# Graph layer with linear attention and 16 experts: opening loads in order of need, the attention's division in halves, scale and bias folded into W1, output stores on SyncE, early weights between their rows

## The chip, the cores and the metric

The kernel runs on one core of a Trainium2 chip. The metric is the device time of one execution in microseconds (us), lower is better. Engines are named as the profile names them: PE (TensorE matmuls), PEld (its weight loads), DVE (VectorE), ACT (ScalarE), POOL (GpSimd) and SP (SyncE, which here only issues DMAs).

## The reference

`x` has 3125 nodes of 256 features; there are 53125 edges, sorted by target; there are 16 experts with 512 hidden features, and each node goes to two of them. Cut to what matters:

```python
xn = layernorm(x)
# 1. graph: every node sums its weighted neighbours
agg = segment_sum(edge_weight[:, None] * xn[src], dst)          # 3125 x 256
gnn = agg @ gnn_W.T + gnn_b
# 2. mixer: linear attention over all nodes, 8 heads of 32
Q, K, v = elu(xn @ Wq) + 1, elu(xn @ Wk) + 1, (xn @ Wv) / N
KV  = einsum('shd,shv->hdv', K, v)
Z   = 1 / (einsum('lhd,hd->lh', Q, K.sum(0)) + 1e-6)
msg = layernorm((einsum('lhd,hdv,lh->lhv', Q, KV, Z) * N) @ Wm) * g1 + b1
h   = relu(concat([xn, msg]) @ W1) @ W2
mix = layernorm(h) * g2 + b2
x = x + gnn + xn + mix
# 3. experts: top 2 of 16, renormalised
y = layernorm(x)
p = softmax(y @ gate_w + gate_b); weights of the two largest, divided by their sum
out = x + sum over the two experts of weight * ((silu(y @ w1[e]) * (y @ w2[e])) @ w3[e])
```

## The kernel before

The nodes are cut into 25 tiles of 125 nodes (128 rows with padding). All of x lies in SBUF as `x_all` from the opening to the end, and results are added into it. PE does almost all of the work, in this order of stages:

1. **Opening and row tiles** (0 to about 116 us). One loop over the 25 tiles. `normed(t + 1)` normalises the next tile on DVE (`xn`, L408), transposes it on PE (L417) and copies it to `xnT` on ACT (L418). `projected(t)` multiplies by `wcat` (gnn_W, Wk and Wv side by side; L426, L428), forms `k_sb` with two ACT operations and one of DVE (L434), and stores the projected neighbours' rows `y`. `summed(t - 1)` adds K times v into `pkv` (L450). The loads of x come in six batches (`LOADS`), the moments and reciprocal roots in four (`BATCHES`; `rsqrt` is 14 small DVE instructions in a chain).
2. In the same loop a generator `windows()` is advanced piece by piece: it finds, for each five target nodes, where their edges begin, gathers a window of 128 edges each (indirect DMAs issued by POOL), and turns them into `keys` and `wgts`, with DVE work on 125x640 elements per piece. `LISTS` says after the `xn` of which tile how many pieces are taken. The piece that needs the gathered windows begins with the cast to `src_f` (L282).
3. From tile `HOT` on, `adjacency()` builds dense pieces of the adjacency matrix from keys and weights: a compare (`one`, L331) and a product (`wone`, L336) on DVE, 12 matmuls on PE (L351), a copy on ACT (L354), a store to HBM (`adj_d`) from SP.
4. **End of the KV sum and the mixer groups** (about 116 to 580 us). The tiles are taken in seven groups of four or three. `asked()` is a generator for the queries of one group: two projections (L466) with exp and relu, then the sums for the division (`ksum`, L476), an ACT copy (L478), the reciprocal (L479) and the product (L480) on DVE. `mixer()` then multiplies by `kvw` (L616), normalises on DVE (`mw`, L624), transposes (L628), applies the scale g1 and the bias b1 on ACT while copying to `mT` (L630), multiplies by `w1` (L639) and `w2` (L650). `queries[g + 1]` is advanced inside group g, and between the steps of a group the loop at the end adds `adjacencies` and `messages` (the products of the stored adjacency with y, L600), as many as `groups` says: (tiles, adjacencies, messages).
5. **Last messages and routing** (about 580 to 720 us). `last_messages(t)` adds the last part of the neighbours (L715, L717) and stores the rows of x to `out` (L719, issued by ACT). Gates and routing of batches of tiles run between them (`gate`: the transposed copy xT on ACT, L773, and the logits, L776, L777). `early_blocks()` gives the first six blocks of experts' work their lists, asks for the first weights (`wt`) and gathers their rows (`xb`) from POOL.
6. **Experts** (about 720 to 1047 us). Blocks of up to 256 lanes: rows gathered, transposed (L964) and copied (`xTb`, L967), multiplied (L978), silu and product (L985), L1004, and added to `out` by indirect DMAs of POOL (L1008).

Each engine executes its instructions in order. The order is chosen when the kernel is built, by a scheduler that follows the dependencies and the `issue_after` marks in the code; one instruction that waits holds back everything behind it on its engine. DMAs issued by one engine's queue start in the order of issue. The pool `a_ps` has PSUM tiles under the names "big" (two buffers) and "tok" (three).

Of the kernel before, what the change touches and what calls it, by code (L numbers as in the profile page):

```python
# [55 lines left out]
LISTS = {1: 1, 6: 1, 7: 2, 8: 2, 13: 1, 14: 1, 15: 1}  # L56
AHEAD = {1: (2, 5), 2: (5, 9), 3: (9, 12), 4: (12, 15), 6: (15, 17), 9: (17, 21), 10: (21, 25)}
HOT = 17
# [4 lines left out]
def tile_gps_layer(ctx: ExitStack, tc: tile.TileContext, a: dict, out: bass.AP):  # L63
# [12 lines left out]

    def row_bcast(src, n, name, pool=const):
        t = pool.tile([P, n], F32, name=name)
        nc.gpsimd.dma_start(t, bass.AP(tensor=src.tensor, offset=src.offset, ap=[[0, P], [1, n]]))
        return t  # L80
# [18 lines left out]
    def stats(mv, src):  # L99
        st = small.tile([P, 6], F32, name="bn_st")  # L100
        nc.vector.bn_stats(st, src)
        nc.vector.bn_aggr(mv, st)
# [18 lines left out]


# [6 lines left out]
    nc.gpsimd.memset(ones, 1.0)  # L129
    before = const.tile([V, V], F32, name="before")  # L130
# [31 lines left out]
    for batch in LOADS[1:3]:  # L162
        load_x(nc.sync, *batch)
    load_x(nc.scalar, *LOADS[3])
# [19 lines left out]
    nc.gpsimd.dma_start(g1, a["g1"])  # L184
    b1 = const.tile([128, 2], F32, name="b1")
    nc.gpsimd.dma_start(b1, a["b1"])
# [3 lines left out]
    nc.gpsimd.dma_start(gate_w, a["gate_w"].rearrange("(k p) e -> p k e", p=128))  # L190
    cb = w_mix.tile([P, C], F32, name="cb")
    nc.gpsimd.tensor_tensor(cb, b2, gnn_b, op=ALU.add)
# [33 lines left out]
    def windows():  # L226

        thr = prep.tile([V, GC], F32, name="thr")
        nc.gpsimd.iota(thr, pattern=[[GN * V, GC]], base=0, channel_multiplier=GN,
                       allow_small_or_imprecise_dtypes=True)  # L230
# [33 lines left out]
        for i in range(GC):  # L264
# [8 lines left out]
            nc.gpsimd.indirect_dma_start(out=win[:, i, :, :].rearrange("p e w -> p (e w)"), out_offset=None,  # L273
                                         in_=a["edges"][:, :],
                                         in_offset=bass.IndirectOffsetOnAxis(ap=start_i[:, at], axis=0))
            if i < GC - 1:
                yield
        nc.sync.dma_start(first_d.rearrange("(i r) o -> r (i o)", r=V), start_i)
# [106 lines left out]
    def deviations(t0, t1):  # L385
        ready[t0] = rsqrt(mv[:, t0:t1, 1], t1 - t0)
        nc.vector.tensor_scalar(by[:, t0:t1], ready[t0], 1.0, None, op0=ALU.add)
        nc.vector.scalar_tensor_tensor(less[:, t0:t1], mv[:, t0:t1, 0], -1.0, ready[t0], op0=ALU.mult, op1=ALU.mult)

    def moments(t0, t1):  # L390

        for i in range(t0, t1):
            stats(mv[:, i, :], x_all[:, i, :])
        for batch in BATCHES:
            if batch[1] == t1:
                deviations(*batch)

    pieces = windows()
    with tc.issue_after(next(pieces).ins):
        moments(*BATCHES[0])  # L400
    def normed(t):
# [8 lines left out]
        with tc.issue_after(ins.ins):  # L410
            for _ in range(LISTS.get(t, 0)):
                next(pieces, None)
            if t in AHEAD:
                moments(*AHEAD[t])
# [38 lines left out]
    groups = ((4, 4, 0), (4, 23, 5), (4, 23, 7), (4, 23, 7), (3, 23, 7), (3, 23, 7), (3, 23, 2))  # L453
# [3 lines left out]
    def asked(t0, nt):  # L457
# [5 lines left out]
        for c in range(2):  # L463
# [9 lines left out]
            yield  # L473
        for c in range(2):
            pz = a_ps.tile([128, 512], F32, name="big")
            nc.tensor.matmul(pz[:, :w], lhsT=ksum[:, c, :], rhs=qT[:, c, :w], start=True, stop=True)  # L476
            z = mix.tile([128, GROUP * P], F32, name="eq")
            nc.scalar.activation(z[:, :w], pz[:, :w], AF.Copy, bias=ATT_EPS / N, scale=1.0 / N)  # L478
            nc.vector.reciprocal(z[:, :w], z[:, :w])  # L479
            nc.vector.tensor_tensor(qT[:, c, :w], qT[:, c, :w], z[:, :w], op=ALU.mult)  # L480
            yield
# [5 lines left out]
    for t in range(NT):  # L487
# [10 lines left out]
        if t >= HOT:  # L498
            adjacencies(1 if t == HOT else 2)
# [21 lines left out]
    for c in range(2):  # L521
        pw = a_ps.tile([P, C], F32, name="tok", bufs=3)
        nc.tensor.matmul(pw, lhsT=kvT[:, c, :], rhs=wm[:, c, :], start=True, stop=True)
        nc.scalar.copy(kvw[:, c, :], pw)
    for _ in range(2):
        next(queries[1])
# [79 lines left out]
    def mixer(t0, nt, qT, following):  # L606
# [16 lines left out]
        for i in range(nt):  # L623
# [5 lines left out]
            for k in range(2):  # L629
                nc.scalar.activation(mT[:, k, i * P : (i + 1) * P], ptr[:, k, :], AF.Identity,  # L630
                                     bias=b1[:, k : k + 1], scale=g1[:, k : k + 1])
# [3 lines left out]
        for j in range(4):  # L635
# [5 lines left out]
            nc.scalar.activation(hT[:, j, :w], ph[:, :w], AF.Relu)  # L641
# [66 lines left out]
    def last_messages(t):  # L708
# [10 lines left out]
        nc.scalar.dma_start(out[t * V : (t + 1) * V, :], x_all[:V, t, :])  # L719
# [211 lines left out]
    SYNC = mybir.DependencyInfo(mybir.DependencyClass.Sync, mybir.DependencyReason.DATA)  # L931

    class Block:
# [8 lines left out]
        def rows(self):  # L942
            self.xb = ex.tile([LANES, 2, XW], F32, name="xb", bufs=4)
            for r in range(self.n):
                at = self.of[0][:, self.u + r : self.u + r + 1]

                tc.keep_in_program_order(nc.gpsimd.indirect_dma_start(
                    out=self.xb[:, r, :], out_offset=None, in_=self.given,
                    in_offset=bass.IndirectOffsetOnAxis(ap=at, axis=0)))

# [105 lines left out]
    def early_blocks():  # L1056
# [21 lines left out]
        behind = blocks[1].weights(nc.gpsimd, behind)  # L1078
# [10 lines left out]
        blocks[2].weights(nc.gpsimd, behind)  # L1089
        for block in blocks:  # L1090
            block.of = of
        for block in blocks[:4]:
            block.rows()
# [173 lines left out]
```

## Time and profile before

| | us |
|---|---|
| three runs | 1047.76, 1048.47, 1049.95 |
| median of the runs | 1048.47 |
| the profiled execution | 1049.14 |
| its span, first to last instruction | 1047.47 |
| PE busy | 1009.6 (96%) |
| DVE busy | 654.2 (62%) |
| ACT busy | 271.2 (26%) |
| POOL busy | 214.4 (20%) |
| mean granted clock of PE | 0.990 |

All durations and start times in the text come from the one profiled execution. "Granted clock" is the share of full speed that PE was given; "idle before <-releaser" names what ended an engine's idle time. Lines such as L434 are lines of the kernel before.

### The profile page before, as it was taken

What the parts mean: (1) busy time and instruction counts of PE and PEld (TensorE: products, weight loads), DVE (VectorE), ACT (ScalarE), POOL (GpSimd) and SP (SyncE); (2) the same over time, 40 slices, a digit from 0 to 9 for tenths busy, and PEclk for the clock granted to TensorE, in tenths of its full rate; (3) what the DMA queues carried; (4) which work ended last, traced back from release to release, by engine and by line L of the source; (5) the groups of instructions that cost most, each with busy time, mean ns of one, the idle gap of its engine ahead of it and who ended that gap; (6) DMA issues with size and microseconds to landing.
All of it is one profiled execution on the core that took longest, in us unless ns stands there. A gap on an engine that the chain in (4) does not pass through costs nothing.

```text
span 1047.5 us, 16216 instructions
## 1 busy us (share of the span) xinstructions
PE 1009.6 (96%) x5990; PEld 810.3 (77%) x5990; DVE 654.2 (62%) x1721; ACT 271.2 (26%) x588; POOL 214.4 (20%) x198
## 2 busy tenths in 40 slices
PE   7899999999999999999999999998999999999995
PEld 5567656686687787887877888887888888888884
DVE  8868589799698887965698248686942222222221
ACT  3466534223324232222142000103111111111110
POOL 5220000104110000000000001012545444445542
PEclk9899999999999999999999999999999999999998
DMA  8324103444343344443444555573756767677662
GB/s 227 74 96 172 61 31 120 143 140 148 116 140 142 121 161 151 167 176 140 143 181 142 175 165 159 166 263 118 201 161 182 246 203 222 183 219 220 196 203 27
DMA packets 70373, 165.08 MB, mean 158 GB/s; under 512 B 11091, under 2 KB 29934, under 8 KB 66314
## 3 DMA queue, kind: packets, MB, share of 16 engines
q1 hardware_dynamic: 50422, 134.24, 37.5%
q0 software_dynamic: 15520, 25.04, 10.6%
q10 hardware_dynamic: 4340, 4.64, 1.4%
q8 instruction: 50, 0.82, 0.3%
q14 instruction: 41, 0.34, 0.1%
HBM read 105.85 MB, written 58.00 MB: 156 GB/s over the span
## 4 chain that ended last, share of the span: by engine, by line
PE 72%; DVE 12%; issue 2%; ACT 1%; another core or an unknown queue 1%; DMA 0%; POOL 0%; ACTq 0%; POOLq 0%; DVEq 0%
PE ph L978 18%; PE pb L600 13%; PE po L1004 10%; PE big L639 7%; PE po L715 7%; PE pa L351 6%; PE tok L650 4%; DVE wone L336 2%; DVE one L331 1%; PE pa L600 1%; PE ptr L964 1%; PE big L466 1%; PE tok L616 1%; DVE wone L346 1%; PE big L476 1%
## 5 line engine op out<-in xcount | busy, mean ns | idle before, releaser
L978 PE MATMUL ph<-xTb,wt 128*128 128x256 f32 (+2 forms) x992 | 204.5, 355 | 3.4 <-ACT xTb L967 3.4
L978 PEld LDWEIGHTS ph<-xTb,wt 128*128 128x128 f32 x992 | 171.5, 190 | 27.4 <-ACT xTb L967 8.3
L600 PE MATMUL pb<-y_early,nbr 128*128 128x256 f32 x736 | 170.7, 382 | 0.4 <-DVE x_all L602 0.4
L336 DVE TENSOR_TENSOR wone<-one,wgts 128x1536 bf16<-128x1536 bf16 x150 | 141.7, 954 | 34.7 <-PE pa L351 34.5
L351 PEld LDWEIGHTS <-one 128*128 128x128 bf16 x1875 | 117.5, 97 | 40.9 <-issue 19.7
L600 PEld LDWEIGHTS pb<-y_early,nbr 128*128 128x128 f32 x736 | 135.4, 190 | 17.2 <-DVE x_all L602 1.0
L354 ACT COPY adj<-pa 128x512 f32<-128x512 f32 (+1 forms) x157 | 91.8, 586 | 185.7 <-PE pa L351 166.5
L351 PE MATMUL pa<-wone,one 128*128 128x128 bf16 x1875 | 130.6, 218 | 2.4 <-ACT adj L354 1.1
L985 DVE TENSOR_TENSOR hid<-hid,ph 128x512 f32<-128x512 f32 (+2 forms) x62 | 38.3, 618 | 144.8 <-PE ph L978 138.6
L1004 PE MATMUL po<-wt,hid 128*128 128x256 f32 (+1 forms) x456 | 115.2, 385 | 0.8 <-DVE yb L1007 0.8
L715 PE MATMUL po<-y_late,nbr 128*128 128x256 f32 x450 | 103.9, 385 | 0.5 <-DVE x_all L602 0.5
L331 DVE TENSOR_TENSOR one<-iota,keys 128x1024 bf16<-128x1024 bf16 x150 | 101.4, 696 | 0.6 <-POOL wgts L313 0.6
L1008 POOL DMA_INDIRECT out<-yb,to_l x45 | 70.9, 1575 | 114.6 <-DMA out<-yb,to_l 52.2
L715 PEld LDWEIGHTS po<-y_late,nbr 128*128 128x128 f32 x450 | 84.2, 192 | 11.4 <-DVE x_all L602 0.9
L1004 PEld LDWEIGHTS po<-wt,hid 128*128 128x128 f32 (+1 forms) x456 | 79.1, 184 | 17.6 <-DVE yb L1007 5.5
L984 ACT ACTIVATE hid<-ph 128x512 f32<-128x512 f32 (+2 forms) x62 | 33.6, 542 | 208.0 <-PE ph L978 206.1
L677 POOL TENSOR_TENSOR x_all<-x_all,cb 128x256 f32<-128x256 f32 x25 | 27.0, 1100 | 200.5 <-DVE x_all L602 145.5
L1007 DVE TENSOR_SCALAR yb<-po,sh 128x256 f32<-128x256 f32 (+1 forms) x57 | 27.5, 482 | 57.3 <-PE po L1004 55.3
L728 POOL IOTA rev<- 125x16 f32 x1 | 0.1, 149 | 296.6 <-DMA nbr<-adj_d 296.6
L426 PE MATMUL big<-wcat,xnT 128*128 128x512 f32 x100 | 49.4, 616 | 1.9 <-DMA wcat<-in_Wk 1.9
L639 PE MATMUL big<-xnT,w 128*128 128x512 f32 (+1 forms) x112 | 50.0, 559 | 0.7 <-ACT eq L478 0.7
L639 PE MATMUL big<-mT,w 128*128 128x512 f32 (+1 forms) x112 | 47.8, 549 | 1.8 <-ACT mT L630 1.8
(283 smaller groups left out, 1185.8 us busy)
## 6 DMA issues: line engine op xcount, KB each, us to landing
wt<-in_w SPq DMA_DIRECT2D x28, 1536.0 KB, 6.9
adj_d<-adj SPq DMA_DIRECT2D x156, 256.0 KB, 2.1
nbr<-adj_d SPq DMA_DIRECT2D x25, 576.0 KB, 4.3
nbr<-adj_d SPq DMA_DIRECT2D x50, 256.0 KB, 2.6
nbr<-adj_d SPq DMA_DIRECT2D x25, 512.0 KB, 3.4
wt<-in_w POOLq DMA_DIRECT2D x3, 1536.0 KB
out<-x_all ACTq DMA_DIRECT2D x25, 125.0 KB
xn_d<-rows POOLq DMA_DIRECT2D x4, 629.9 KB
```

Source lines behind the costliest of these rows:

```text
L331: nc.vector.tensor_tensor(one.rearrange("p b h e j -> p (b h) e j"), iota_2[:, None, :, :].to_broadcast(shape), ql.rearrange("p b h j -> p ...
L336: nc.vector.tensor_tensor(wone, one[:, :, 1:2, :, :].to_broadcast(shape), w[:, :, :, None, :].to_broadcast(shape), op=ALU.mult)
L351: nc.tensor.matmul(pa[:, j, :], lhsT=one[:, j // 2, 0, :, j % 2], rhs=wone[:, j // 2, i, :, j % 2], start=(i == 0), stop=(i == 2))
L354: copied = nc.scalar.copy(rows[:, :n, :], pa[:, :n, :])
L426: nc.tensor.matmul(pyk, lhsT=xnT[:, k, cols], rhs=wcat[:, k, : 2 * C], start=(k == 0), stop=(k == 1))
L600: nc.tensor.matmul(pb[:, i, :], lhsT=rows[:, k - t0, :], rhs=y_of(k), start=(k == t0 and i == 0), stop=(k == t1 - 1), skip_group_check=True)
L639: nc.tensor.matmul(ph[:, :w], lhsT=w1[:, k, j * 128 : (j + 1) * 128], rhs=rhs, start=(k == 0), stop=(k == 3))
L650: nc.tensor.matmul(po, lhsT=hT[:, j, i * P : (i + 1) * P], rhs=w2[:, j, :], start=(j == 0), stop=(j == 3))
L715: last = nc.tensor.matmul(pg, lhsT=rows[:, k - t0, :], rhs=y_of(k), start=(k == t0), stop=(k == t1 - 1))
L978: last = nc.tensor.matmul(p[:, m, :w], lhsT=self.wt[:, i, k * F + at : k * F + at + 128], rhs=self.xT[:, k, :w], start=(k == 0), stop=(k = ...
L1004: last = nc.tensor.matmul(po[:n_r, r, :], lhsT=self.hid[:, k, r * LANES : r * LANES + n_r], rhs=self.wt[:, 2, k * C : (k + 1) * C], start= ...
L1008: made.append(nc.gpsimd.indirect_dma_start(out=out[:, :], out_offset=bass.IndirectOffsetOnAxis(ap=at, axis=0), in_=yb[:n_r, r, :], in_offs ...
```

## The change

It has these parts:

- **Opening.** The seven loads of small constants and the sum `cb` on POOL are put in a list, and issued after the last window gather. `thr` is made early. The third and fourth batches of x are both issued by SP, and wait until the moments of the first two tiles are done (the fourth was on ACT's queue). `by` and `less`, two small factors, are computed after the first `xn` of a batch and not before it.
- **Lists.** The last three pieces of `windows()` come after tiles 14, 15 and 16 instead of 13, 14 and 15; `HOT` is 18 instead of 17, and every tile from there on has two adjacencies (tile 17 had one). The first mixer group has five adjacencies instead of four.
- **Division in halves.** `asked()` issues both sums first, and then works on the first two tiles (256 columns) of both halves of the features, then on the rest: ACT copy, reciprocal and product for each.
- **Scale and bias in W1.** After the KV sum, eight matmuls of one column compute `h_bias` (the lower half of W1 times b1), and POOL multiplies the lower half of `w1` by g1. `mT` is then one plain copy for each tile, and the relu takes `h_bias` as its bias.
- **Stores.** The 25 stores of the rows of x to `out` are issued by SP.
- **Early weights.** POOL issues the weights of block 1 after the rows of blocks 0 and 1, and those of block 2 after the rows of block 2.

```diff
 
-LISTS = {1: 1, 6: 1, 7: 2, 8: 2, 13: 1, 14: 1, 15: 1}
+LISTS = {1: 1, 6: 1, 7: 2, 8: 2, 14: 1, 15: 1, 16: 1}
 AHEAD = {1: (2, 5), 2: (5, 9), 3: (9, 12), 4: (12, 15), 6: (15, 17), 9: (17, 21), 10: (21, 25)}
-HOT = 17
+HOT = 18
 GROUP = 4
...
 
+    later = []
+
     def row_bcast(src, n, name, pool=const):
         t = pool.tile([P, n], F32, name=name)
-        nc.gpsimd.dma_start(t, bass.AP(tensor=src.tensor, offset=src.offset, ap=[[0, P], [1, n]]))
+        later.append((t, bass.AP(tensor=src.tensor, offset=src.offset, ap=[[0, P], [1, n]])))
         return t
...
     nc.gpsimd.memset(ones, 1.0)
+    thr = const.tile([V, GC], F32, name="thr")
+    nc.gpsimd.iota(thr, pattern=[[GN * V, GC]], base=0, channel_multiplier=GN, allow_small_or_imprecise_dtypes=True)
     before = const.tile([V, V], F32, name="before")
...
         nc.scalar.dma_start(wcat[:, :, i * C : (i + 1) * C], a[name].rearrange("(k p) o -> p k o", p=128))
-    for batch in LOADS[1:3]:
-        load_x(nc.sync, *batch)
-    load_x(nc.scalar, *LOADS[3])
+    load_x(nc.sync, *LOADS[1])
     wq = w_mix.tile([128, 2, C], F32, name="wq")
...
     g1 = const.tile([128, 2], F32, name="g1")
-    nc.gpsimd.dma_start(g1, a["g1"])
+    later.append((g1, a["g1"]))
     b1 = const.tile([128, 2], F32, name="b1")
-    nc.gpsimd.dma_start(b1, a["b1"])
+    later.append((b1, a["b1"]))
     g2 = row_bcast(a["g2"], C, "g2", w_mix)
...
     gate_w = const.tile([128, 2, NE], F32, name="gate_w")
-    nc.gpsimd.dma_start(gate_w, a["gate_w"].rearrange("(k p) e -> p k e", p=128))
+    later.append((gate_w, a["gate_w"].rearrange("(k p) e -> p k e", p=128)))
     cb = w_mix.tile([P, C], F32, name="cb")
-    nc.gpsimd.tensor_tensor(cb, b2, gnn_b, op=ALU.add)
 
...
 
-        thr = prep.tile([V, GC], F32, name="thr")
-        nc.gpsimd.iota(thr, pattern=[[GN * V, GC]], base=0, channel_multiplier=GN,
-                       allow_small_or_imprecise_dtypes=True)
         heads = prep.tile([V, V], F32, name="heads")
...
             nc.vector.tensor_copy(start_i[:, at], start_f[:, at])
-            nc.gpsimd.indirect_dma_start(out=win[:, i, :, :].rearrange("p e w -> p (e w)"), out_offset=None,
+            gathered = nc.gpsimd.indirect_dma_start(out=win[:, i, :, :].rearrange("p e w -> p (e w)"), out_offset=None,
                                          in_=a["edges"][:, :],
...
                 yield
+        with tc.issue_after(gathered.ins):
+            for place, what in later:
+                nc.gpsimd.dma_start(place, what)
+            nc.gpsimd.tensor_tensor(cb, b2, gnn_b, op=ALU.add)
         nc.sync.dma_start(first_d.rearrange("(i r) o -> r (i o)", r=V), start_i)
...
 
-    def deviations(t0, t1):
-        ready[t0] = rsqrt(mv[:, t0:t1, 1], t1 - t0)
-        nc.vector.tensor_scalar(by[:, t0:t1], ready[t0], 1.0, None, op0=ALU.add)
-        nc.vector.scalar_tensor_tensor(less[:, t0:t1], mv[:, t0:t1, 0], -1.0, ready[t0], op0=ALU.mult, op1=ALU.mult)
+    def factors(t0, t1, rstd):
+        nc.vector.tensor_scalar(by[:, t0:t1], rstd, 1.0, None, op0=ALU.add)
+        nc.vector.scalar_tensor_tensor(less[:, t0:t1], mv[:, t0:t1, 0], -1.0, rstd, op0=ALU.mult, op1=ALU.mult)
 
...
         for i in range(t0, t1):
-            stats(mv[:, i, :], x_all[:, i, :])
-        for batch in BATCHES:
-            if batch[1] == t1:
-                deviations(*batch)
+            found = stats(mv[:, i, :], x_all[:, i, :])
+        for t0, end in BATCHES:
+            if end == t1:
+                ready[t0] = rsqrt(mv[:, t0:t1, 1], t1 - t0)
+        return found
 
...
     with tc.issue_after(next(pieces).ins):
-        moments(*BATCHES[0])
+        found = moments(*BATCHES[0])
+
+    for batch in LOADS[2:4]:
+        tc.add_manual_dep(load_x(nc.sync, *batch).ins, found.ins.name, SYNC, reason="loads in the order of need")
+
     def normed(t):
...
         with tc.issue_after(ins.ins):
+            for batch in BATCHES:
+                if t == batch[0]:
+                    factors(*batch, rstd)
             for _ in range(LISTS.get(t, 0)):
...
 
-    groups = ((4, 4, 0), (4, 23, 5), (4, 23, 7), (4, 23, 7), (3, 23, 7), (3, 23, 7), (3, 23, 2))
+    groups = ((4, 5, 0), (4, 23, 5), (4, 23, 7), (4, 23, 7), (3, 23, 7), (3, 23, 7), (3, 23, 2))
     asked_for = []
...
             yield
+
+        pz = []
         for c in range(2):
-            pz = a_ps.tile([128, 512], F32, name="big")
-            nc.tensor.matmul(pz[:, :w], lhsT=ksum[:, c, :], rhs=qT[:, c, :w], start=True, stop=True)
-            z = mix.tile([128, GROUP * P], F32, name="eq")
-            nc.scalar.activation(z[:, :w], pz[:, :w], AF.Copy, bias=ATT_EPS / N, scale=1.0 / N)
-            nc.vector.reciprocal(z[:, :w], z[:, :w])
-            nc.vector.tensor_tensor(qT[:, c, :w], qT[:, c, :w], z[:, :w], op=ALU.mult)
+            p = a_ps.tile([128, 512], F32, name="big")
+            nc.tensor.matmul(p[:, :w], lhsT=ksum[:, c, :], rhs=qT[:, c, :w], start=True, stop=True)
+            pz.append((p, mix.tile([128, GROUP * P], F32, name="eq")))
+        for part in (slice(0, 2 * P), slice(2 * P, w)):
+            for c, (p, z) in enumerate(pz):
+                nc.scalar.activation(z[:, part], p[:, part], AF.Copy, bias=ATT_EPS / N, scale=1.0 / N)
+                nc.vector.reciprocal(z[:, part], z[:, part])
+                nc.vector.tensor_tensor(qT[:, c, part], qT[:, c, part], z[:, part], op=ALU.mult)
             yield
...
         if t >= HOT:
-            adjacencies(1 if t == HOT else 2)
+            adjacencies(2)
         last, *taken_on = projected(t)
...
         nc.scalar.copy(kvw[:, c, :], pw)
+
+    pb1 = a_ps.tile([P, C], F32, name="tok", bufs=3)[:, :4]
+    for j in range(4):
+        for k in range(2):
+            nc.tensor.matmul(pb1[:, j : j + 1], lhsT=w1[:, 2 + k, j * 128 : (j + 1) * 128], rhs=b1[:, k : k + 1],
+                             start=(k == 0), stop=(k == 1))
+    h_bias = w_mix.tile([128, 4], F32, name="h_bias")
+    nc.vector.tensor_copy(h_bias, pb1)
+    for k in range(2):
+        nc.gpsimd.tensor_scalar(w1[:, 2 + k, :], w1[:, 2 + k, :], g1[:, k : k + 1], None, op0=ALU.mult)
     for _ in range(2):
...
                 nc.tensor.transpose(ptr[:, k, :], mw[:, i, k * 128 : (k + 1) * 128], ident)
-            for k in range(2):
-                nc.scalar.activation(mT[:, k, i * P : (i + 1) * P], ptr[:, k, :], AF.Identity,
-                                     bias=b1[:, k : k + 1], scale=g1[:, k : k + 1])
+            nc.scalar.copy(mT[:, :, i * P : (i + 1) * P], ptr)
             yield
...
                                  start=(k == 0), stop=(k == 3))
-            nc.scalar.activation(hT[:, j, :w], ph[:, :w], AF.Relu)
+            nc.scalar.activation(hT[:, j, :w], ph[:, :w], AF.Relu, bias=h_bias[:, j : j + 1])
             yield
...
         stats(mv_g[:, t, :], x_all[:, t, :])
-        nc.scalar.dma_start(out[t * V : (t + 1) * V, :], x_all[:V, t, :])
+        nc.sync.dma_start(out[t * V : (t + 1) * V, :], x_all[:V, t, :])
         return last
...
         yield
-        behind = blocks[1].weights(nc.gpsimd, behind)
 
...
         of = yield from lists(col, EARLY_TILES, 2 * EARLY, "e")
-        blocks[2].weights(nc.gpsimd, behind)
         for block in blocks:
             block.of = of
-        for block in blocks[:4]:
-            block.rows()
+        for block in blocks[:2]:
+            behind = block.rows()
+        blocks[1].weights(nc.gpsimd, behind)
+        behind = blocks[2].rows()
+        blocks[2].weights(nc.gpsimd, behind)
+        blocks[3].rows()
         early.extend(blocks)
```

`SYNC` is a dependency on a semaphore, which the third and fourth loads of x get on the last instruction of `moments`.

More of the change, by code (lines that the diff above doesn't have):

```diff
@@ L101, in stats @@
         nc.vector.bn_stats(st, src)
-        nc.vector.bn_aggr(mv, st)
+        return nc.vector.bn_aggr(mv, st)
     def rounded(to, src, by, shift):
@@ L120, in placed @@
         return t, r, row
+    SYNC = mybir.DependencyInfo(mybir.DependencyClass.Sync, mybir.DependencyReason.DATA)
     ident = const.tile([128, 128], F32, name="ident")
@@ L930, in tile_gps_layer @@
     added = []
-    SYNC = mybir.DependencyInfo(mybir.DependencyClass.Sync, mybir.DependencyReason.DATA)
     class Block:
@@ L945, in rows @@
                 at = self.of[0][:, self.u + r : self.u + r + 1]
-                tc.keep_in_program_order(nc.gpsimd.indirect_dma_start(
+                last = tc.keep_in_program_order(nc.gpsimd.indirect_dma_start(
                     out=self.xb[:, r, :], out_offset=None, in_=self.given,
                     in_offset=bass.IndirectOffsetOnAxis(ap=at, axis=0)))
+            return last
         def weights(self, queue, behind):
```

## The prediction

> **What bounds the kernel now.** I read the page first, then the waits of PE, then the granted clock in short windows, then the timelines of DVE and ACT at the larger waits. The page says that PE is the bound nearly everywhere:
>
> ```profile
> PE 1009.6 (96%) x5990; PEld 810.3 (77%) x5990; DVE 654.2 (62%) x1721; ACT 271.2 (26%) x588; POOL 214.4 (20%) x198
> ```
>
> The span is 1047.5 us, so PE is idle for 37.9 us in all, some 10 of it in the tail, where the last adds to the output land. An edit off PE can gain only PE's waits and the stretches in which PE is busy at a lower clock. The waits, largest first (line, what it waited for, us in total, times, longest):
>
> ```profile
> PE tok L628 <- DVE mw L624: 4.3, 5, 1.3
> PE ph L978 <- ACT xTb L967: 3.4, 1, 3.4
> PE pkv L450 <- DVE k_sb L434: 3.2, 1, 3.2
> PE tok L616 <- DVE qT L480: 2.2, 1, 2.2
> PE tok L417 <- DVE xn L408: 2.2, 2, 1.5
> PE big L426 <- DMA wcat<-in_Wk: 1.9, 1, 1.9
> ...
> PE big L639 <- ACT mT L630: 1.8, 1, 1.8
> PE ph L776 <- ACT xT L773: 1.4, 2, 1.2
> ...
> PE big L639 <- ACT eq L478: 0.7, 1, 0.7
> ```
>
> The windows (from:to, length, busy time of PE, PEld, DVE, ACT and POOL, granted clock, DMA share) show that three of these waits cost twice. The first row is an idle stretch, the next two and the last two are what followed such stretches:
>
> ```profile
> 44.23:47.44 3.21, 0.00 (x0) 0.03 (x1) 2.89 (x6) 0.91 (x3) 0.00 (x0) 0.82 0.14 48
> 46.27:49.69 3.42, 2.25 (x7) 1.79 (x8) 3.42 (x7) 0.37 (x1) 0.00 (x0) 0.50 0.01 2
> 49.69:53.10 3.41, 3.41 (x6) 1.69 (x5) 3.41 (x7) 0.58 (x3) 0.00 (x0) 0.50 0.00 0
> 128.19:131.60 3.41, 3.41 (x10) 2.66 (x9) 2.33 (x8) 1.51 (x5) 0.00 (x0) 0.50 0.00 0
> 660.67:664.09 3.42, 3.42 (x11) 2.89 (x11) 0.17 (x1) 0.23 (x1) 0.00 (x0) 0.50 0.34 118
> ```
>
> At 0.50 PE does half the work, so these stretches lose 5.66/2 = 2.83 us, 1.7 us and 1.7 us. Their edges lie 3.41 us apart on one grid. A stretch at 0.50 came when the grid window before it held about 2.0 us of idle PE (twice), once with 1.2 us of idle and a few 16-column matmuls. It did not come after gaps of 1.9 us and less, nor after the 3.36 us at 717, which lay half in one grid window and half in the next.
>
> **Lists one tile later (LISTS 13 to 16, HOT 18).** The cause of the 3.2 us wait is in DVE's timeline:
>
> ```profile
> 40.51 0.41 DVE L408 TENSOR_SCALAR xn<-x_all,mv,rs_y 128x256 f32<-128x256 f32 x1
> 44.45 0.59 DVE L282 CAST src_f<-win 125x640 f32<-125x640 int32 x1 [3.53 <-DMA win<-in_edges,start_i]
> ```
>
> DVE sits on the window gather while k_sb (L434), which PE needs, is queued behind. The change puts the cast behind the xn of the next tile, one tile period (3.25 us of PE work) later: of 3.53 us of wait some 0.3 is left, and k_sb had about that much slack. PE gets back 3.22 + 2.83 = 6.05; I take 5.75. Low end 3: the gather lands later, since the wait is for its last packets; high end 6.05. HOT 18 moves one adjacency (12 L351 matmuls, 0.85 us) from tile 17 into mixer group 0; for PE that is even.
>
> **End of the KV sum and mixer group 0 (116 to 160 us).** Before, two L479 reciprocals of 3.35 us run one behind the other (119.2 to 126.0) with their products, PE waits 2.19 us at L616, then comes a stretch at 0.50 (1.7), then 0.7 for eq and 1.8 for mT: 6.4 us. After, both L476 matmuls come first and the reciprocals go in halves, about 1.7 each by width; the tiles of the first half are ready after two, near 123.1, and of the second near 127.2. New costs on PE: both "big" buffers are held by the two sums until ACT has copied them (0.65 at the next query's projection, 0.85 at its second sum); 16 passes of N=1 for h_bias, 0.11 each by the spacing of the narrow matmuls at L776 and L964, 1.8 in all; and the adjacency above (0.85). Replaying PE's order with these durations I get L616 at 127.35, with no wait and full clock, and the last of group 0 (L650) at 151.2 instead of 153.8. That is 2.6, and 3.45 with the adjacency that tile 17 saved; I take 3.4, from 1.5 (a stretch at 0.50 stays) to 4.4. The product of W1 with g1 is two POOL operations on 128x512; 128x256 takes 1.1 us there (L677), so about 4.4, and POOL is idle in 130 to 160. One mT copy of 128x256 (0.37) replaces two of 0.46: ACT gains 0.5 us per tile, and where ACT is not waited for that is nothing.
>
> **Later groups.** The four half reciprocals now follow one upon another: by the order of DVE, 9.4 us lie between one wone (L336) and the next in a group of four tiles. PE has queued in that time the two sums, three adjacencies, eight L600 matmuls and four L639: about 9.0. So PE may wait 0.4 to 1.2 us in two groups, less in those of three tiles; DVE's extra instructions add 0.2 per group. I take -1.0, from 0 to -3. The 4.3 us of L628 stay.
>
> **Opening.** With x(5,10) and x(10,15) held until the moments of tile 1 (5.1 us), Wk lands before xnT is ready, so the first projection starts at about 9.05 and not 10.85. But the next step is bound by DVE: xn of tile 2 comes at 14.59. What moves it: the L92 that took 0.85 instead of 0.17 while POOL added cb; the wait of cmp_h for thr (0.1); by and less, now behind xn (0.15). Hence 13.7, and PE goes on at 14.2 instead of 15.15: 0.95. The two gaps of 1.9 and 1.5 become one of 2.5. By the rows above, a gap of 2.5 us holds 2.0 us or more within one grid window for 56% of the grid's positions, and then costs 1.7; so I take 0.95 - 0.85 = 0.1, from -0.75 to 0.95. The Trainium skill ("TensorE: Matmul & The Clock Gate", Part 1) says that the clock halves after at least one idle window of about 3.4 us. The trace disagrees: 2.0 us were enough. By that rule the opening would be worth 0.95 and nothing else in the sum would change. The seven constants' DMAs (0.54 to 0.76 us of POOL each, 4.2 in all) now follow the last window gather, at 36 to 41 us, where POOL waits anyway; their first readers come after 120 us.
>
> **Stores on SyncE.** Before, ACT held the finished xT copy behind a store that waited for DVE's x_all:
>
> ```profile
> 657.83 0.27 ACTq L719 DMA_DIRECT2D out<-x_all  x1
> 658.20 0.65 ACT L773 COPY xT<-ph 128x256 f32<-128x256 f32 x2 [2.16 <-DVE rs_y L96]
> ```
>
> PE waited 1.2 us for it and ran the next window at 0.50: 1.2 + 1.7 = 2.9, all of which goes. On SP, the nbr load of three tiles on is queued behind the store, which waits for x_all; three tiles of 3.9 us are 11.7, a load lands in 4.3. Bounds 1.2 to 2.9; I take 2.9.
>
> **Weights between rows on POOL.** Before, three loads of 1536 KB were asked for at 697 to 700, and the rows' gathers started at 708. Around 712 to 720 the chain of waits has
>
> ```profile
> 712.39 7.33 another core or an unknown queue
> ```
>
> and PE lost 3.4 us at L978, although the rows had landed. I can't tell whether the burst did that or an accident of that execution. The change spreads the loads; none is needed before 730. I take 0, up to 3.4.
>
> **Sum.** 5.75 + 3.4 - 1.0 + 0.1 + 2.9 + 0 = 11.15. The profiled execution took 1049.14 (span 1047.47 and 1.67 outside it), 0.67 above the median of the runs. 1049.14 - 11.15 = 1038.0, and 1037.3 counted from the median. I say 1037.5. A measurement of this kernel tells about 0.2% (2.1 us) from no change; I count 1046.4 to 1050.6 as the same.
>
> **Rivals.** (1) *The gather lands a tile later too.* Its descriptors share the engines with the later x loads and y stores, and the 8.5 us from the last issue (35.9) to the last landing (44.4) are not explained by its 192 KB. DVE then waits 2 to 3.5 us again, PE loses 3 to 6 of the 5.75: 1041 to 1043.5. Against it: nothing in the change issues anything ahead of that gather on POOL. (2) *The hole at 717 goes as well, and the opening meets a good grid:* 3.4 + 0.85 more, 1033. For it: DMA engines were 99% busy for ten microseconds before. Against it: the rows were there. (3) *Slower: the clump of reciprocals starves PE in each of the five later queries.* DVE is busy 51.3 of 60 us in 240 to 300, so a delay isn't made up quickly. If PE waits 2.2 us, which trips the clock for 1.7 more, five times 3.9 is 19.5: 1049.1 - 12.15 + 19.5 = 1056.5. It decides from 12.15/5 = 2.4 us per group on. Against it: DVE waited 34.5 us for PE at L336 in this stage, so it runs ahead, and 9.4 stands against 9.0. (4) *Several of the waits come back elsewhere and nothing is seen*: PE's new waits for "big" buffers, a stretch at 0.50 in group 0 and in the opening, and rival 1 together cost 11: about 1047.
>
> **Numbers.** The forecast 0.62 (1034.5 to 1041), rival 1 0.16, rival 2 0.09, rival 3 0.08, rival 4 0.05. Faster 0.87, same 0.05, slower 0.08. The range 1031 to 1044 holds the forecast and rivals 1 and 2 and leaves out some 0.15.
>
> **What would show it.** In the changed kernel's waits of PE: L434 at the KV product gone or under 0.5; the L616 row and the mT row gone; a single row of some 2.5 us for xn in the opening, and none for Wk; no ACT row at the gate; the clock at 1.00 through 46 to 53, 128 to 132 and 660 to 664. I am wrong if DVE still shows about 3 us at the cast of src_f, if PE has new rows over 1.5 us for wone or for ACT's eq copy in 160 to 500 us, or if new windows at 0.50 appear there.

## The result, and the profile after

The changed kernel took 1037.36 us (median of 4 runs, 1036.32 to 1038.03), the kernel before 1048.99 (4 runs, 1047.76 to 1049.95); the ratio is 0.989, interval 0.9877 to 0.9903. The forecast was 1037.5. The profiled executions took 1038.03 (span 1036.2) and 1049.14 (span 1047.5). The first part of the page after:

```profile
PE 1007.1 (97%) x6006; PEld 809.3 (78%) x6006; DVE 655.3 (63%) x1750; ACT 263.9 (25%) x577; POOL 216.1 (21%) x200
```

The span is 11.3 us shorter, of which 8.8 is idle time of PE. Its busy time fell by only 2.5: the stretches at 0.50 ahead of the tail cost 6.2 before (half of the 12.5 us in which PE was busy in them) and 1.7 after, but 16 narrow matmuls of 1.84 us are new. The waits of PE in the changed kernel (line numbers are now those of the changed code: L428 is the transpose that was L417, L461 was L450, L641 was L616, L653 was L628, L662 was L639, L1001 was L978):

```profile
PE tok L653 <- DVE mw L649: 4.2, 5, 1.3
PE tok L428 <- DVE less L391: 2.6, 1, 2.6
...
PE tok L641 <- DVEq L559: 1.0, 1, 1.0
PE tok L428 <- DVE xn L416: 0.9, 1, 0.9
...
PE ph L1001 <- issue: 0.8, 1, 0.8
PE big L489 <- ACT eq L493: 0.8, 1, 0.8
...
PE ph L799 <- issue: 0.7, 1, 0.7
...
PE big L662 <- ACT mT L654: 0.5, 1, 0.5
...
PE ph L799 <- DVE rs_y L98: 0.4, 1, 0.4
```

The rows for Wk and for k_sb are gone, the hole before the first expert block has shrunk, and the opening has one gap of 2.6 us. At the gate (L799 was L776) PE no longer waits for xT; 0.4 us for DVE is left of 1.2. DVE's timeline shows why k_sb is no longer late; the cast follows the next tile's xn without a wait:

```profile
42.67 0.41 DVE L416 TENSOR_SCALAR xn<-x_all,mv,rs_y 128x256 f32<-128x256 f32 x1 [0.41 <-PE tok L428]
43.05 0.60 DVE L286 CAST src_f<-win 125x640 f32<-125x640 int32 x1
```

The windows (same columns as before) show the clock at full speed in the stretches that ran at 0.50, and a new stretch behind the gap of the opening:

```profile
11.73:15.15 3.42, 0.85 (x5) 0.47 (x4) 3.21 (x17) 1.31 (x5) 1.97 (x2) 1.00 0.60 177
15.13:18.54 3.41, 3.41 (x6) 1.63 (x5) 3.41 (x17) 0.68 (x3) 2.80 (x3) 0.50 0.60 192
46.27:49.69 3.42, 3.42 (x16) 2.26 (x15) 3.42 (x8) 2.11 (x7) 0.00 (x0) 1.00 0.17 56
49.69:53.10 3.41, 3.41 (x16) 2.21 (x15) 3.41 (x7) 2.00 (x6) 0.00 (x0) 1.00 0.15 49
128.19:131.60 3.41, 2.17 (x14) 1.32 (x14) 3.31 (x11) 2.00 (x7) 0.00 (x0) 1.00 0.00 0
```

Where the time went can be read by taking the start of the same instruction in both traces. Before minus after: 1.07 us behind (the changed kernel is later) at the xnT copy of tile 3; 5.25 ahead at tile 14; 5.88 at ksum; 7.70 at the first L650 result of group 0; 7.36 at the end of the groups; 10.32 at the 15th of the last messages; 11.88 at the first expert block; 11.91 at the last block.

So by stage, with the forecast in brackets: opening -1.07 (0.1); lists +6.32 (5.75); tile 17's adjacency +0.63 and group 0 +1.82, together 2.45 (3.4); later groups -0.34 (-1.0); stores +2.96 (2.9); weights +1.56 (0); the tail gave back 0.6. The sum of the forecast's terms, 11.15, stands beside a measured difference of the profiled executions of 11.11. The experiments show that not all of this agreement is earned. In the table below, one of the five timings of fill4 (2115.7 us) is left out of its ratio; what disturbed it is not known.

### The profile page after: what moved, and what is told of

Same layout as the page of the kernel before. It is cut to its first block, busy times and chain, and to the rows that moved or that the text cites. A ratio compares the mean times of both kernels' runs of the same rounds, so it can differ in the third digit from the quotient of the medians.

```text
span 1036.2 us, 16279 instructions
## 1 busy us (share of the span) xinstructions
PE 1007.1 (97%) x6006; PEld 809.3 (78%) x6006; DVE 655.3 (63%) x1750; ACT 263.9 (25%) x577; POOL 216.1 (21%) x200
## 4 chain that ended last, share of the span: by engine, by line
PE 71%; DVE 10%; issue 1%; POOL 0%; ACT 0%; POOLq 0%; DVEq 0%; ACTq 0%
PE ph L1001 18%; PE pb L625 13%; PE po L1027 10%; PE po L738 8%; PE pa L355 6%; PE big L662 6%; PE tok L673 3%; DVE wone L340 2%; PE ptr L987 1%; PE pa L625 1%; PE big L477 1%; DVE one L335 1%; PE ph L799 1%; DVE wone L350 1%; PE big L489 1%
## 5 line engine op out<-in xcount | busy, mean ns | idle before, releaser
L1001 PE MATMUL ph<-xTb,wt 128*128 128x256 f32 (+2 forms) x992 | 204.5, 355 | 0.8 <-issue 0.8
L1001 PEld LDWEIGHTS ph<-xTb,wt 128*128 128x128 f32 x992 | 171.5, 190 | 24.9 <-ACT xTb L990 4.5
L627 DVE TENSOR_TENSOR x_all<-x_all,pb 128x512 f32<-128x512 f32 (+1 forms) x37 | 24.3, 655 | 41.8 <-PE pb L625 41.8
L662 PE MATMUL big<-xnT,w 128*128 128x512 f32 (+1 forms) x112 | 49.8, 556 | 0.0
```

Of the source, the lines that this page charges most:

```text
L662: nc.tensor.matmul(ph[:, :w], lhsT=w1[:, k, j * 128 : (j + 1) * 128], rhs=rhs, start=(k == 0), stop=(k == 3))
L1001: last = nc.tensor.matmul(p[:, m, :w], lhsT=self.wt[:, i, k * F + at : k * F + at + 128], rhs=self.xT[:, k, :w], start=(k == 0), stop=(k = ...
```

## The experiments

Each kernel ran beside the kernel before, in three sets of runs: the first four rows of the table, the next four, and the last four. In them the kernel before took 1045.8, 1046.1 and 1045.2, some 3 us less than in the result. The changed kernel itself ran only in the last set, at 1037.02, 0.9921 (0.9905 to 0.9936) of the kernel before. Differences are therefore taken from ratios (times 1046); with both intervals such a difference is uncertain by about 2.2 us. Smaller ones are read from the traces, at the same instruction, and rest on one execution of each kernel. "Undone" means: the changed kernel with that part put back.

| kernel | median, us | ratio to before | interval |
|---|---|---|---|
| u_lists, lists undone | 1041.59 | 0.9959 | 0.9945 to 0.9973 |
| u_open, opening undone | 1037.96 | 0.9921 | 0.9905 to 0.9937 |
| u_halves, halves undone | 1036.32 | 0.9908 | 0.9893 to 0.9924 |
| u_fold, fold into W1 undone | 1043.96 | 0.9983 | 0.9970 to 0.9996 |
| u_stores, stores undone | 1040.42 | 0.9949 | 0.9935 to 0.9962 |
| u_weights, early weights undone | 1036.71 | 0.9910 | 0.9896 to 0.9925 |
| fill_open, 16 matmuls in the gap | 1038.33 | 0.9927 | 0.9914 to 0.9939 |
| before_again, the kernel before, one profiled run | 1046.43 | - | - |
| after_again, nothing undone | 1037.02 | 0.9921 | 0.9905 to 0.9936 |
| u_mixer, halves and fold undone | 1035.56 | 0.9909 | 0.9894 to 0.9924 |
| fill4, 4 matmuls in the gap | 1035.99 | 0.9911 | 0.9894 to 0.9928 |
| best4, halves undone and 4 matmuls | 1035.62 | 0.9910 | 0.9896 to 0.9925 |

**u_lists.**

```diff
-LISTS = {1: 1, 6: 1, 7: 2, 8: 2, 14: 1, 15: 1, 16: 1}
+LISTS = {1: 1, 6: 1, 7: 2, 8: 2, 13: 1, 14: 1, 15: 1}
-HOT = 18
+HOT = 17            # with one adjacency in tile 17 and four in group 0
```

> The changed kernel with only the lists put back (pieces after tiles 13, 14, 15, HOT 17, four adjacencies in group 0). Theory: the tile of delay is what hides the window gather. DVE again reaches the cast of src_f one tile early, near 40.6, and waits 1.5 to 3 us; PE waits about as long at L461 for k_sb, and the clock falls to 0.50 behind it. From the changed kernel's 1037.4 to 1041 to 1044. Rival: the gather lands earlier because the constants and the x loads no longer stand before it, so the shift is worth little: no DVE wait over 1 us at the cast, and 1037 to 1038.5.

Measured: 0.9959 against 0.9921, that is 4.0 us. From the waits of DVE (15 to 60 us) and of PE (8 to 70 us):

```profile
DVE src_f L286 <- DMA gate_b<-in_gate_b: 3.9, 1, 3.9
```
```profile
PE pkv L461 <- DVE k_sb L445: 3.0, 1, 3.0
```

The wait, PE's stall and one window at 0.50 (49.1 to 52.5) are back. In the trace the kernel is 5.4 us behind the changed one at ksum, 5.1 at the end of group 0 and 6.0 at the end of the groups; the last 0.9 arises in group 1, where PE waits 0.6 for an `nbr` load, as it does in u_open (0.5), so it is not shown to belong to the lists. The theory holds; the rival falls. The releaser named is a constant's DMA, which shares POOL's queue with the gather; the cast reads only the gather.

The other profiles say the same. In the three with the lists of before (before, before_again, u_lists), DVE waits 3.5 to 4.1 us at the cast and PE 3.0 to 3.8 for k_sb. In the eleven with the tile of delay, DVE waits 0 to 3.4, and PE not at all but for 1.4 in after_again. Where it waited, the cast starts at 44.5 to 45.8 with the opening of before (three profiles) and at 43.3 to 45.2 with the new one (nine). The ranges overlap, so that the gather comes earlier is not shown; the tile of delay hides the wait.

**u_open.**

```diff
-    load_x(nc.sync, *LOADS[1])           # batches 2 and 3 behind the moments
+    for batch in LOADS[1:3]:
+        load_x(nc.sync, *batch)
+    load_x(nc.scalar, *LOADS[3])
...                                       # constants first, thr late, by and less before xn
```

> The changed kernel with only the opening put back (constants first on POOL, thr late, x loads unordered, by and less before xn). Theory: the opening is worth 0.6 us at the third tile without a clock stretch and cost 1.1 in the profiled run because the single gap of 2.6 us brought 3.4 us at 0.50; put back, the two gaps of 1.9 and 1.5 return and no stretch: 1036.3 to 1038. Rival: the order of the loads is also what lets the window gather land in time; put back, DVE waits 1 to 3 us at the cast again and the time is 1040 to 1044.

Measured: the same ratio as the changed kernel. In the trace it is 0.57 us behind at ksum, where both profiles had one stretch at 0.50 in the opening. The time lies in the range of the theory, but not by its mechanism: PE waits 3.3 us for Wk here (1.9 before), there is no second gap at tile 2, and a stretch at 0.50 did follow, from 12.3. It also loses 1.1 us in group 1, with the wait for `nbr`. The rival falls: 1.9 us of wait at the cast, but no wait of PE.

**u_halves and u_fold.**

```diff
-        for part in (slice(0, 2 * P), slice(2 * P, w)):          # u_halves
+        for c in range(2):      # one sum, ACT copy, reciprocal and product of w columns each
```
```diff
-            nc.scalar.copy(mT[:, :, i * P : (i + 1) * P], ptr)   # u_fold; no h_bias, w1 unscaled
+            for k in range(2):
+                nc.scalar.activation(mT[:, k, i * P : (i + 1) * P], ptr[:, k, :], AF.Identity,
+                                     bias=b1[:, k : k + 1], scale=g1[:, k : k + 1])
```

> The changed kernel with only the division put back to whole tiles of 512 columns; W1 keeps scale and bias. Theory from the changed trace: L641 starts at 121.8, after the second half is done (121.0), not after the first (117.1), because PE passes the branch at L559 only when DVE has reached it; so the halves bring nothing at this place, and the time is within 0.6 us of 1037.4. Rival, the one I predicted by: the halves are what removes the wait and the stretch at 0.50 in group 0, and without them 2 to 3.5 us come back: 1039.5 to 1041.

> The changed kernel with only the scale and bias put back on ACT (no h_bias matmuls, two ACT operations per mT tile). Theory: the 1.84 us of 16 narrow passes cost nothing, since PE would stand at the branch until DVE's reciprocals are done (121.8) in any case; without them PE waits 2.6 to 2.8 us there, the clock falls for 3.4 us in about two of three executions, and the wait for mT grows from 0.5 to 1.5 or more: 1038.5 to 1041.5. Rival: PE is the bound, so taking 1.84 us off it gains 1 to 1.8: 1035.6 to 1036.4.

Measured: u_halves is not slower, 0.9908. Its median lies 1.1 us below 1037.4, outside the 0.6 of the theory but within the intervals; its profile has no stretch in the opening, which puts it 0.75 ahead at ksum. Between ksum and the end of the groups it gains 0.3 us on the changed kernel. The halves bring nothing, as the trace after suggests: the first L641 starts at 121.8, behind the second half, because PE is let past the branch by DVE's sequencer (L559), and DVE gets there only after all four reciprocals and h_bias. DVE and PE of the changed kernel:

```profile
117.04 3.36 DVE L494 RECIPROCAL eq<-eq 128x256 f32<-128x256 f32 x2
120.31 0.69 DVE L495 TENSOR_TENSOR qT<-qT,eq 128x256 f32<-128x256 f32 x2
...
121.81 3.90 PE L641 MATMUL tok<-kvw,qT 128*128 128x256 f32 x16 [0.95 <-DVEq L559]
```

u_fold is 6.5 us slower, and not for the reason that I gave. PE passes the branch at 116.6 and begins L631 (the L641 of the changed kernel) at 118.4, so the first half does help there. But DVE then takes the next group's reciprocals between the steps of this group's rsqrt chain. Parts of DVE's timeline of u_fold:

```profile
127.47 0.16 DVE L96 TENSOR_TENSOR rs_s<-rs_y 128x4 f32<-128x4 f32 x1
127.55 1.74 DVE L494 RECIPROCAL eq<-eq 128x256 f32<-128x256 f32 x1
...
133.49 1.74 DVE L494 RECIPROCAL eq<-eq 128x256 f32<-128x256 f32 x1
...
136.57 1.05 DVE L639 TENSOR_SCALAR mw<-mw,mv_m,rs_y 128x256 f32<-128x256 f32 x3
```

In the changed kernel the same chain runs unbroken and mw comes at 129.4. Here PE waits for it (first line, PE's timeline), and two windows at 0.50 follow:

```profile
137.03 1.54 PE L643 MATMUL tok<-ident,mw 128*128 128x128 f32 x6 [5.44 <-DVE mw L639]
```
```profile
134.39:137.80 3.41, 0.77 (x4) 0.73 (x5) 3.41 (x11) 0.04 (x1) 0.00 (x0) 0.50 0.00 0
137.80:141.22 3.42, 2.89 (x21) 2.38 (x20) 3.42 (x6) 3.36 (x9) 0.00 (x0) 0.50 0.00 0
```

My expectation was right that it would be slower, and wrong on the place, the cause and the size. The rival falls.

**u_mixer.** Both edits undone.

> The changed kernel with both edits of the mixer put back (whole tiles in the division, scale and bias on ACT), lists, opening, stores and weights kept. The half that was put back alone cost nothing (halves) or 6.9 us (fold: DVE had taken the next group's four half reciprocals ahead of the normalisation mw, and PE waited 5.4 us and ran two windows at 0.50). Theory: the 6.9 us belong to the halves without the fold, an order that the scheduler chose; with both put back the order of before returns, with its waits at L616 (2.2), eq (0.7) and mT (1.8), and the two edits together are worth 1.5 to 2.6: 1038.3 to 1040. Rival: what hides the division is the fold itself; then this costs 6 to 7 us like the fold alone: 1042.5 to 1044.

Measured: 1035.56, 0.9909; not slower but 1.3 us faster by the ratios, which lies within their intervals; the traces agree: between ksum and the end of the groups it gains 1.29 us on the changed kernel (0.82 in group 0, 0.47 later). The waits of PE in its group 0 (105 to 160 us):

```profile
PE tok L627 <- DVE qT L491: 1.5, 1, 1.5
PE big L650 <- ACT mT L641: 0.8, 1, 0.8
PE big L650 <- ACT eq L489: 0.7, 1, 0.7
```

These waits, without the halves and the fold, come to 3.0 us against 4.7 of the same three rows before, and the 1.84 us of the 16 narrow matmuls are saved. Theory and rival both fall: of the mixer's two edits nothing is left as a gain, together they cost about 1.3. The 6.5 us of u_fold belong to the halves without the fold, an order of DVE. Part of what shortens group 0 is what I had costed as even: the adjacency moved there from tile 17. In u_lists, which has one fewer in group 0 (0.85 us of PE), the stretch from ksum to the first L650 is shorter than in the changed kernel by 0.28 and not 0.85; the other 0.57 fills a wait.

**u_stores.**

```diff
-        nc.sync.dma_start(out[t * V : (t + 1) * V, :], x_all[:V, t, :])
+        nc.scalar.dma_start(out[t * V : (t + 1) * V, :], x_all[:V, t, :])
```

> The changed kernel with the output stores put back on ACT. Theory: the store at the gate holds xT again for 1.2 us and the clock falls behind it: 2.9 us more at the tile after the gate in the trace, time 1039 to 1040.5. Rival: the gap was a matter of the moment at which the gate fell; now that everything comes 7.4 us earlier the clock grid lies elsewhere, and only 1.2 or less returns: 1037.5 to 1038.6.

Measured: 0.9949, 2.9 us more. ACT's timeline and the windows around it:

```profile
649.98 0.27 ACTq L742 DMA_DIRECT2D out<-x_all  x1
650.35 0.65 ACT L796 COPY xT<-ph 128x256 f32<-128x256 f32 x2 [2.10 <-DVE rs_y L98]
```
```profile
648.50:651.44 2.94, 1.78 (x14) 1.38 (x14) 2.69 (x15) 0.65 (x2) 0.00 (x0) 1.00 0.88 295
651.44:654.85 3.41, 3.41 (x12) 2.85 (x12) 0.34 (x2) 0.37 (x1) 0.00 (x0) 0.50 0.49 175
```

Against the changed kernel it loses 2.95 us between the first and the 15th of the last messages, 1.2 by the gap and the rest by the stretch. The theory holds.

**u_weights and before_again.**

```diff
-        for block in blocks[:2]:
-            behind = block.rows()
-        blocks[1].weights(nc.gpsimd, behind)
...
+        behind = blocks[1].weights(nc.gpsimd, behind)      # before the lists
...
+        blocks[2].weights(nc.gpsimd, behind)               # before all rows
+        for block in blocks[:4]:
+            block.rows()
```

> The changed kernel with the early weights put back in one burst before the rows. Theory: the burst of 4.7 MB is what held back PE before the first block; the hole of about 3.4 us before the first ph matmul returns, against 1.5 in the changed kernel: 1.5 to 2 us more at the first xTb copy, time 1038.5 to 1039.5. Rival: the 3.4 us of before were an accident of one execution, and PE idles 1.5 or less there: 1037 to 1037.8.

> The kernel before, unchanged, for a second profile. If the hole of 3.4 us before the first ph matmul comes from the burst of weights, it is there again, 3 to 3.6 us, with the same long step of an unknown queue; if it was an accident of that execution, it is under 2 us. The three stretches at 0.50 should return behind the same three waits, the one at 660 only if the grid lies alike.

Measured: u_weights is not slower (0.9910), and PE's wait there is 0.7. The same in the second profile of the kernel before (690 to 740 us), which has the burst:

```profile
PE ph L978 <- ACT xTb L967: 0.7, 1, 0.7
```

So the 3.4 us are no fixed cost of the burst. Whether one execution or the whole set of the result had them is open: only one of its four runs of before was profiled. The changed kernel's own first profile had a smaller one, the two rows "issue" of 0.7 and 0.8: between the 21st and the 25th of the last messages it loses 0.95 us to every other variant. The edit itself is worth nothing that shows. Two of before's three stretches came back, at 48.1 (two windows) and at 659.1. The one behind L616 did not, though PE waited 2.2 us there again.

**fill_open and fill4.**

```diff
+        if t == 0:
+            pf = bank_a()
+            with tc.issue_after(last.ins):
+                for i in range(16):              # fill4: range(4)
+                    nc.tensor.matmul(pf[:, i % 4, :], lhsT=ones, rhs=ones, start=True, stop=True)
```

> The changed kernel with 16 matmuls of ones behind the first projection, on a spare PSUM tile that nobody reads: they fill 1.8 us of the 2.6 us in which PE waits for xn of tile 2, and change nothing else. Theory: the granted clock goes by idle time within a window; with 0.8 us idle no stretch at 0.50 follows, PE loses 1.7 us less in each execution in which the gap lay well within a window: the profile shows 1.00 through 12 to 20 us, and the median is 0.8 to 1.7 lower, 1035.7 to 1036.6. Rival: the stretch has another cause (the DVE or DMA load of the opening), or falls in few executions: 1037 to 1037.8.

> The changed kernel with 4 matmuls of ones (8 passes, 0.9 us) after the first projection instead of the 16 of the run before, which took 3.7 us, not 1.8, as a matmul of fp32 makes two passes: they pushed tile 2 back by 1.0 us and moved a k_sb behind the chain of rsqrt. Here they leave 1.6 us of the gap idle, and DVE's order is nearly that of the changed kernel. Theory: no stretch at 0.50 in the opening; xnT of tile 3 at 18.3 instead of 20.0; of that 1.7 about 1.0 is given back by tile 14, where DVE waits for the gather; the median falls by 0.3 to 0.8 and the runs lie closer together. Rival: nothing measurable, as the gap was already harmless in 2 of 6 profiles and slack eats the rest: within 0.3 of the changed kernel.

Measured: neither profile has a stretch at 0.50 ahead of the tail. The 16 matmuls took 3.7 us instead of 1.8 and moved k_sb behind a chain of rsqrt (PE waited 1.6 for it), so fill_open lost more than it won. fill4 leaves 1.7 us of the gap; its xnT of tile 3 comes at 18.3 against 20.0, but at ksum only 0.8 of that is left, since DVE waits 1.5 us at the cast. Its median is 1.0 below the changed kernel of the same set, with intervals that overlap: the direction is as expected, the size not settled.

**after_again and best4.**

> The changed kernel once more, beside the others of this call on the same chip, because the kernel before was 1045.8 and 1046.1 in the two calls so far against 1049.0 in the result. Theory: the changed kernel does not move as much, since it has fewer waits behind DMAs: 1036.3 to 1038, so the ratio here is 0.990 to 0.993. Its second profile should lack the hole of 1.0 us before the first expert block (707), which none of the seven variants showed; then an accident like the 3.4 us of before. Rival: it comes down by 3 us as well, to 1034 to 1035.

> The changed kernel with whole tiles in the division (which alone gave 1036.3) and the 4 matmuls in the opening gap. If both add up: 0.5 to 1.2 below the changed kernel of this call. If the halves do help and the 1036.3 was only a good grid: the same as the changed kernel or 0.3 above it.

Measured: the changed kernel is at 1037.02 while the kernel before moved from 1049.0 to 1045.2, so here the change is worth 8.2 us. The hole before the first block is absent (0.7). But its cast waits, unlike in the first profile:

```profile
45.17 0.59 DVE L286 CAST src_f<-win 125x640 f32<-125x640 int32 x1 [3.39 <-DMA gate_b<-in_gate_b]
```

and PE loses 1.4 us at L461. best4 is at 1035.62, 1.1 below by the ratios, again within the intervals; in the trace it gains 0.4 on fill4 between ksum and the end of the groups, the cost of the halves. u_mixer with the 4 matmuls was not run.

## Why the prediction was right, point by point

The time came out. The mechanism was right for the lists and the stores and wrong for the mixer, and that the total fits even so is luck in part.

**Lists: right.** 5.75 forecast, 6.3 in the pair of profiles, 4.0 by the ratios when undone. Rival 1 exists in part: the gather still lands as late as 45.2, and in one of two profiles of the changed kernel PE paid 1.4 us for it. DVE's wait in that profile, 3.4 us, is what I had named as a sign of being wrong (about 3 us at the cast): the delay took away most of what PE pays for the wait, not always the wait.

**Stores: right**, in mechanism and size: 2.9 forecast, 2.96 in the pair, 2.95 when undone.

**Opening: mechanism and odds right, the size too high.** The first projection starts at 9.11 (9.05 forecast), tile 2's xn at 13.69 (13.7). The gap of 2.4 to 2.6 us brought a stretch at 0.50 in five of the eight profiles with this opening and no filler (after, u_lists, u_fold, u_weights, u_mixer, not in after_again, u_halves, u_stores); 56% was worked out, which eight profiles cannot tell from other odds near a half. But 0.1 was forecast, -0.75 at worst, and the pair shows -1.07. That xn took 0.69 us against 0.42 before, so PE went on at 14.53 and not 14.2; without a stretch the opening is worth 0.58 at tile 3 (after_again against before) and not 0.95. What I left out: of the 1.65 to 1.75 us that a stretch costs at tile 3, u_halves, u_stores, fill4 and best4, which have none, keep only 0.7 to 0.9 at tile 14, and after_again keeps nothing, since the gather holds DVE there anyway.

**Weights: right at 0.** The 1.56 us in the pair of profiles are two holes of different size, which undoing the edit does not bring back. So half of rival 2, that the hole at 717 goes as well, came true in the pair, but not through the edit.

**End of the KV sum and group 0: the step that failed.** It gave 3.4 to the halves and the fold, by a replay in which L616 would find its first tiles early and mT would no longer be waited for. Measured between ksum and the end of the groups: the two edits cost 1.3 us (u_mixer against the changed kernel). Three things in the step were wrong. The first half's tiles are of no use while PE stands at the branch until DVE has done all four reciprocals. The adjacency was costed as even, but 0.57 of its 0.85 us fill a wait of group 0. u_mixer, which has it and neither of the mixer's edits, is 1.07 us faster in this stretch than the second profile of before. And the 1.7 us at 0.50 behind L616 were entered as a certain loss: with the same wait of 2.2 us, the second profile of before has no such stretch. Two smaller readings were off without moving the sum: the product of W1 with g1 took 3.1 us on POOL, not 4.4 (one operation of 5.5 us lifts the mean of L677 to 1.1; the median is 0.73), and DVE's 34.5 us of waiting at L336 are of the whole kernel, 31.2 from 116 to 600 us. With the two edits at -1.3 and 0.57 for the adjacency in place of 3.4 and -1.0, my sum would have been 8.0.

**Later groups:** -1.0 forecast, -0.34 in the pair; -0.47 by u_mixer. Rival 3, the clump of reciprocals that starves PE in every group, did not happen; where it did happen was u_fold, once, in group 0.

**The sum** came out because the excess of the mixer step stands against what this profile of before had lost and the second had not: the hole at 717, of which 1.56 us are left in the pair, and the stretch at 128 (1.7). That is luck. It does not explain the medians: all four runs of before in the result lie 1.6 us or more above its later medians, and why is not known. Against the lower times of before in the later sets, the change is worth 8.2 us and not 11.6. The parts do not settle that figure. With 6.0 for the lists (end of the groups), 0.6 for the opening, 2.95 for the stores, -1.3 for the mixer and 0 for the weights they make 8.2; with 5.1 for the lists (end of group 0) 7.4; with 4.0 for the lists and nothing for the opening, as the ratios have them, 5.6. The second profiles of the two kernels are 9.35 apart at the last block.

**The clock.** The Trainium skill ("TensorE: Matmul & The Clock Gate", Part 1) asks for at least one idle window of about 3.4 us. The runs disagree: 2.0 us were enough, as the prediction read, and the gap of 1.1 to 1.2 us at the gate, with 16-column matmuls around it, was followed by a stretch at 0.50 in each of the three profiles that had it.

Beyond the odds, the traces show what decides. All stretches of one profile begin whole multiples of 3.41 us apart (in the first of before 24, 180 and 291 windows after the first, the last being the tail). If that grid is laid over the gaps of all fourteen profiles between the first matmul and the tail, twelve windows hold 2.0 to 3.1 us of one gap, and each was followed by 0.50; of the windows at full clock that hold 1.9 us or less, only the three at the gate were. The wait at L616 has 2.01 us in one window in the first profile of before and 1.74 in the second; the 2.57 us of the opening lie in one window in `after` and are cut into 0.67 and 1.90 in after_again; the 3.3 us in the opening of before_again, which no stretch followed, into 1.54 and 1.76.

## What to carry to other kernels

A wait on a late transfer costs most when it stands in an in-order queue ahead of something else that the bound engine needs; one step of delay for the piece that waits, or another queue for it, was worth more here than any edit that made work smaller. Before a replay is believed, follow every engine through barriers and branches too, and ask what the scheduler will put into the place that is freed. Take a second profile before entering a rare hole or a clock stretch as a gain: the hole of 3.4 us and the stretch of 1.7 behind L616 were not there the next time.

## What the runs showed of the hardware

Where DVE waited for the window gather, the cast behind it started between 43.3 and 45.8 us (twelve profiles), a spread larger than most of the edits are worth. Whether a gap of 2.2 to 3.3 us lowers the clock changes from one execution to the next of the same code, with the place of the gap on the grid of 3.41 us.
